# Copies for depthwise convolutions that carry a pair of row shifts per transfer

## The chip, the cores and the metric

The kernel runs on one core of one Trainium2 chip. The metric is the device time of one execution in microseconds. The kernel before took 11327.4 us, the median of three runs (11325.69 to 11348.05).

## The reference

A batch of 64 images of 96 channels and 28 x 28 pixels passes four layers.

```python
# layer 0 (k = 5): routed experts; layers 1 and 3 (k = 3): the same shape without routing and gating
out = act(bn1(conv1x1(x, 96 -> 576)))           # silu in layer 0, relu in layers 1 and 3
out = act(bn2(depthwise_conv(out, k x k)))      # layer 0: a kernel per image, mixed from 4 experts
...                                             # layer 0: squeeze-and-excite gate on out
x   = x + bn3(conv1x1(out, 576 -> 96))          # layer 0: weights mixed from 4 experts
# layer 2, on each quarter (14 x 14) of the image: group norm, conv1x1, 3 x 3 depthwise,
# four-direction selective scan, group norm, gate, channel gate, x + y
```

The depthwise convolutions of layers 0, 1 and 3 work on 576 channels of 28 x 28 pixels: for each channel, the sum over the k x k taps of a shifted image times a weight.

## The kernel before

**Depthwise convolution as matmuls.** TensorE (PE) does it. A tile `rep` holds, on (k + 1) * cb partitions, cb channels in k + 1 row shifts each (cb = 16 and k = 5, 96 partitions; cb = 32 and k = 3, 128 partitions), for n = 4 (or 2) blocks of channels in the free dimension. The rows of an image are split into even and odd ones, two *slots* `o` of 14 rows, each padded to 16 rows of 32 pixels. With k + 1 row shifts and a weight tile `wd`, a matmul sums the taps of all ky at once for even and odd output rows; the k values of dx are k matmuls that accumulate in one bank of PSUM. The weight tile is made of the taps (`_taps`, lines 98 to 107: one row per lane) and a 0/1 `mask` that says which channel a lane belongs to (`spread_taps`, lines 520 to 529; a lane is a partition of `rep`). Channel and shift of a lane are thus set in three places: the copies into `rep`, the taps, and the mask. Before the change a lane is c * (k + 1) + i, for channel c of the block and shift i.

**From the first convolution to the second.** `expand` (lines 634 to 700) computes the 1x1 convolution of four tiles of 128 channels and one of 64. ScalarE (ACT) evicts each half from PSUM into a bordered tile `pad` in SBUF (128 partitions, 2 slots, 16 rows, 32 pixels), and issues a DMA that stores the tile to the HBM scratch tensor `ex` (lines 670 to 674, 128 rows of 4096 bytes); the fifth tile goes through `hpad` in two stores of 64 channels (`store`, lines 690 to 695, rows of 896 bytes). For k = 3 the slots are stored in reversed order (line 643). There are three tensors `ex`, one for each of the layers 1, 0 and 3 in the loop (line 615), whose last 64 channels are zeroed once in setup.

**The copies.** `rows` (lines 702 to 711) fills `rep` from `ex` with k + 1 DMAs on SyncE's (SP's) queue, one for each row shift i: it reads slot i % 2 from row (i + (k == 3)) // 2 on, 14 rows (1792 bytes), of cb channels in n blocks, and writes the partitions i, i + k + 1, i + 2(k + 1) and so on. `load` (lines 713 to 741) asks for this and for the weight tile `wd`: for layer 0, GpSimd (POOL) spreads the mixed taps of the image (line 735); for layers 1 and 3 a DMA loads tiles that setup spread once (line 738). `depthwise` (lines 743 to 803) has the matmuls (line 756) and the evictions (line 767) of such a unit. An image has 9 units in layer 0 and 5 in each of layers 1 and 3, the last of them with n = 2. `rep` has three buffers, `wd` three, PSUM tiles five (lines 426 to 448).

**The rest.** Layer 2's scans run on VectorE (DVE, lines 1268 to 1278), their sums and products on GpSimd (lines 1231, 1297, 1303), and TensorE collects the states (line 1211). `dd`, `B` and `C` come to it through HBM by SP's DMAs (line 1188). The projections (line 825) end in an addition to `x` on DVE (line 837).

**What sets the order.** A planner in the program (`Plan`, lines 237 to 396) simulates all engines when the kernel is built. Each operation is registered with an engine, an estimated cost, its inputs and outputs, and a due time; `run` places operations greedily by the time they can start and by due time, and emits the instructions of every engine in that order. SP's and ACT's DMAs are such operations, with a cost for the issue, a size and a time to land. On the chip each engine takes its own instructions strictly in that order and waits on semaphores. The image loop (lines 1457 to 1461) runs seven times over a body of eight planned slots; in a slot, layer 2 of one image runs beside layer 1 of the next, layer 0 of the one after that, and layer 3 of the previous one.

Of the kernel before, what the change touches and what calls it, by code (L numbers as in the profile page):

```python
# [9 lines left out]
F32 = mybir.dt.float32  # L10
# [5 lines left out]
P = 128  # L16
C = 96
HID = 576
# [56 lines left out]
def _rows(v):  # L75
    return np.tile(np.asarray(v)[None, :], (P, 1))
# [15 lines left out]
def _parity(cb):  # L92

    lane = np.arange(P) // cb % 2
    return 0.5 * np.stack([lane == 0, lane == 1], axis=1).astype(np.float32)


def _taps(w, cb):


    k = w.shape[1]
    v = w.reshape(HID // cb, cb, k, k)
    out = np.zeros((cb, k + 1, HID // cb, k, 2), np.float32)
    for o in range(2):
        for ky in range(k):
            out[:, ky + o, :, :, o] = v[:, :, ky].transpose(1, 0, 2)
    return out.reshape((k + 1) * cb, HID // cb, k, 2)


def pack_l0(ins):  # L110
    q = {k[len("L0_conv_") :]: np.asarray(v) for k, v in ins.items() if k.startswith("L0_conv_")}
    p = Pack()
    p.add("r_w1", q["r_w1"].T)
    p.add("r_b1", q["r_b1"][:, None])
    p.add("r_w2", q["r_w2"].T)
    p.add("r_b2", _rows(q["r_b2"]))
    p.add("w1", q["exp_w"].T)
    _pack_bn(p, "bn1", q, "bn1_g", "bn1_b", "bn1_m", "bn1_v", _lanes)
    _pack_bn(p, "bn2", q, "bn2_g", "bn2_b", "bn2_m", "bn2_v", lambda a: _groups(a, 16))

    dw = np.zeros((96 + RH, E, 360), np.float32)
    for e in range(E):
        dw[:96, e] = _taps(q["dw_w"][e].reshape(HID, 5, 5), 16).reshape(96, 360)
    dw.reshape(96 + RH, E * 360)[96:, : NG * P] = _groups(q["se_w2"], 16).transpose(2, 1, 0).reshape(RH, NG * P)
    p.add("dw", dw)
    p.add("mask", np.repeat(np.eye(16, dtype=np.float32), 6, axis=0))
    p.add("parity", _parity(16))
    p.add("se_w1", _groups(q["se_w1"].T, 16))
    b1 = np.zeros((96 + RH, 1), np.float32)
    b1[96:, 0] = q["se_b1"]  # L130
    p.add("se_b1", b1)
    p.add("se_b2", _groups(q["se_b2"], 16))
    p.add("bn3gr", _rows(q["bn3_g"]), once=True)
    p.add("bn3vr", _rows(q["bn3_v"]), once=True)
    _pack_bn(p, "bn3", q, "bn3_g", "bn3_b", "bn3_m", "bn3_v", None)
    return p
# [8 lines left out]
def pack_l1(ins, layer):  # L145
    pre = f"L{layer}_conv_"
    q = {k[len(pre) :]: np.asarray(v) for k, v in ins.items() if k.startswith(pre)}
    p = Pack()
    p.add("w1", q["w1"][:, :, 0, 0].T)
    _pack_bn(p, "bn1", q, "g1", "b1", "m1", "v1", _lanes)  # L150
    p.add("dw", _taps(q["wd"].reshape(HID, 3, 3), 32).reshape(P, 18 * 6), once=True)
    p.add("mask", np.repeat(np.eye(32, dtype=np.float32), 4, axis=0), once=True)
    _pack_bn(p, "bn2", q, "g2", "b2", "m2", "v2", _lanes)
    p.add("w3", _lanes(q["w3"][:, :, 0, 0].T))
    p.add("bn3gr", _rows(q["g3"]), once=True)
    p.add("bn3vr", _rows(q["v3"]), once=True)
    _pack_bn(p, "bn3", q, "g3", "b3", "m3", "v3", None)
    return p
# [44 lines left out]
PE, ACT, DVE, POOL, SP = "PE", "ACT", "DVE", "POOL", "SP"  # L203
# [218 lines left out]
class Kernel:  # L422
# [4 lines left out]
        rep=(3, [P, 4, 14, 32]),  # L427
        wd=(3, [P, 768]),
        acc=(15, [P, HALF]),
        h=(2, [P, 4, LSEQ]),  # L430
# [100 lines left out]
    def setup(self, fold):  # L531
        nc = self.nc
# [12 lines left out]
        for e in range(E):  # L545
            t = fold.tile([P, NG, C], F32, name="expert")
# [5 lines left out]
        for layer, c in ((1, c1), (3, c3)):  # L552
            k = f"l{layer}"
            bn1 = self.bn(c, "bn1", 1e-5, k)
            bn2 = self.bn(c, "bn2", 1e-5, k)
            _, b3 = self.bn(c, "bn3", 1e-5, k)
# [3 lines left out]
            for u in range(5):  # L560
                n = 24 if u < 4 else 12
                t = fold.tile([P, 768], F32, name="taps")
# [49 lines left out]
        self.hpad = self.tile([P, 2, 7, 32], "hborder")  # L612
        for t in self.pads + [self.hpad]:
            nc.gpsimd.memset(t, 0.0)
        self.ex = [self.dpool.tile([HID, 2, 16, 32], F32, name=f"ex{i}") for i in range(3)]
        for t in self.ex:
            nc.sync.dma_start(t[4 * P :].rearrange("c o r w -> c (o r w)"), self.pads[0][:64].rearrange("c o r w -> c (o r w)"))
        self.npad = self.ndecay = 0

# [2 lines left out]
    def job(self, layer, t, ex):  # L622

        if layer == 0:
            d = dict(c=self.c[0], bn1=self.bn1_0, bn2=self.bn2_0, b3=self.b3_0)
        else:
            d = self.ir[layer]
        k, cb, func, table = (5, 16, AF.Silu, SILU) if layer == 0 else (3, 32, AF.Relu, None)
        return dict(
            d, layer=layer, x=self.xt[t % 4], keys=[("x", t % 4, h) for h in range(2)],  # L630
            k=k, cb=cb, func=func, table=table, ex=self.ex[ex], exkey=ex, accs=[],
        )

    def expand(self, d):


        nc, pl, x, ex = self.nc, self.plan, d["x"], d["ex"]
        pl.tag = d["layer"]
        w1 = d["c"]("w1")
        scale, bias = d["bn1"]  # L640

        def evict(dst, ps, t):
            dst = dst[:, ::-1] if d["k"] == 3 else dst
            nc.scalar.activation(  # L644
                dst,
                ps()[:, :HALF].rearrange("p (r o w) -> p o r w", o=2, w=28),
                d["func"],
                bias=bias[:, t : t + 1],
                scale=scale[:, t : t + 1],
            )  # L650

        for t in range(4):
            i = self.npad % len(self.pads)
            self.npad += 1
            pad = self.pads[i]
            for h in range(2):
                ps = pl.buf("ps")

                def mm(ps=ps, t=t, h=h):
                    nc.tensor.matmul(  # L660
                        ps()[:, :HALF], w1[:, t * P : t * P + P], x[:, h * HALF : (h + 1) * HALF], start=True, stop=True
                    )

                pl.op(PE, 0.68, mm, r=d["keys"], w=[ps], after=[("pad", i, h)])
                pl.op(
                    ACT, 0.68, lambda ps=ps, t=t, h=h, pad=pad: evict(pad[:, :, 1 + 7 * h : 8 + 7 * h, 2:30], ps, t),
                    r=[ps], w=[("pad", i, h)], table=d["table"],
                )
            flat = "p o r w -> p (o r w)"
            pl.op(  # L670
                ACT, 0.35,
                lambda t=t, pad=pad: nc.scalar.dma_start(ex[P * t : P * t + P].rearrange(flat), pad.rearrange(flat)),
                r=[("pad", i, 0), ("pad", i, 1)], w=[("ex", d["exkey"], t)], nbytes=524288, land=3.5,
            )
            yield
            pl.tag = d["layer"]

        ps, pad = pl.buf("ps"), self.hpad

        def mm():  # L680
            for h in range(2):
                nc.tensor.matmul(
                    ps()[64 * h : 64 * h + 64, :HALF],
                    w1[:, 4 * P :],
                    x[:, h * HALF : (h + 1) * HALF],
                    start=True,
                    stop=True,
                )

        def store():  # L690
            for h in range(2):
                nc.scalar.dma_start(
                    ex[4 * P :, :, 1 + 7 * h : 8 + 7 * h].rearrange("p o r w -> p o (r w)"),
                    pad[64 * h : 64 * h + 64].rearrange("p o r w -> p o (r w)"),
                )

        pl.op(PE, 0.68, mm, r=d["keys"], w=[ps], after=["hpad"])
        pl.op(ACT, 0.68, lambda: evict(pad[:, :, :, 2:30], ps, 4), r=[ps], w=["hpad"], table=d["table"])
        pl.op(ACT, 0.7, store, r=["hpad"], w=[("ex", d["exkey"], 4)], nbytes=230000, land=3.2)
        yield  # L700

    def rows(self, d, rep, ch, n):

        nc, k, cb = self.nc, d["k"], d["cb"]
        src = d["ex"][ch : ch + n * cb].rearrange("(b c) o r w -> c b o (r w)", b=n)
        for i in range(k + 1):
            slot, row = i % 2, (i + (k == 3)) // 2
            nc.sync.dma_start(  # L708
                rep()[i : (k + 1) * cb : k + 1, :n].rearrange("c b r w -> c b (r w)"),
                src[:, :, slot, 32 * row : 32 * row + 448],  # L710
            )

    def load(self, d, u):

        nc, pl, k, cb, layer = self.nc, self.plan, d["k"], d["cb"], d["layer"]
        pl.tag = layer
        if layer == 0:
            ch, n = 64 * u, 4
        else:
            ch, n = P * u, 4 if u < 4 else 2  # L720
        rep, wd = pl.buf("rep"), pl.buf("wd")
        pl.op(
            SP, 0.64 * (k + 1), lambda: self.rows(d, rep, ch, n),
            r=[("ex", d["exkey"], ch // P)], w=[rep], nbytes=(k + 1) * cb * n * 1792, land=4.2 if n == 4 and k == 3 else 2.8,
        )
        m = n * k * 2
# [9 lines left out]
        else:  # L736
            pl.op(
                SP, 0.55, lambda: nc.sync.dma_start(wd()[:, : m * cb], self.taps[layer][u][:, : m * cb]),
                w=[wd], nbytes=P * m * cb * 4,
# [753 lines left out]
```

## Time and profile before

| | |
|---|---|
| median of three runs | 11327.4 us |
| the profiled execution | 11346.26 us |
| its span, first to last instruction | 11344.5 us |
| mean granted TensorE clock | 0.896 |
| DMA issues on SP for `rep` | 6016 |
| DMA busy share of the 16 engines, SP's queue / ACT's queue | 50.1% / 12.6% |
| HBM read / written | 1725.77 MB / 539.49 MB |

The profile is one execution. "PE" is TensorE's matmuls and "PEld" its weight loads. In a group's line stand the source line, the engine, the operation, the tiles (`out<-in`), the shape and the count, then busy time in us and the mean of one in ns, then the idle time of the engine just before these instructions and what ended most of it. A view of waits gives, for each pair of waiter and releaser, the total in us, the number of waits and the longest. "SPq" and "ACTq" are DMA issues on SP's and ACT's queues. The granted clock is the share of TensorE's full speed. The trace also holds a record of every DMA packet (queue, size, start, duration) and of every semaphore update; where the text speaks of records, it means these.

### The profile page before, as it was taken

Reading aid. Unit: us, or ns where it says so; the run is one execution under the profiler, and the core shown is the slowest. Engines: PE = TensorE matmul, PEld = TensorE weight load, DVE = VectorE, ACT = ScalarE, POOL = GpSimd, SP = SyncE. Lnnn points to the kernel's source line nnn. Section 1 sums busy time; section 2 is a strip of 40 time slices with the busy share of each in tenths; the row PEclk is TensorE's granted clock in tenths of the full one; section 3 lists DMA queues with packets and bytes.
Section 4 is the critical chain, followed back from the end, with each engine's and each line's share of the span. In section 5 each row is a group of like instructions: output and inputs, shape, how many; then the busy total and the mean of one; then the engine's idle time right before and its main releaser. Section 6 shows DMA issues by size and latency. Waiting matters only on the chain. (4 is left out here: it accounts for less than half of the span.)

```text
span 11344.5 us, 201157 instructions
## 1 busy us (share of the span) xinstructions
PE 9815.9 (87%) x75526; PEld 4055.5 (36%) x75526; DVE 9261.7 (82%) x8711; ACT 6387.5 (56%) x10605; POOL 8342.3 (74%) x7523
## 2 busy tenths in 40 slices
PE   4689888899989899889998988889988898888895
PEld 2233333333333333333333333333333333333332
DVE  1589887889878888788888888888887888888886
ACT  1365555556555565555555655555555665555653
POOL 5477776777767777687786777777777777767786
PEclk9799998899988999898898999889888899989996
DMA  4366665666656666666666666666666666666662
GB/s 144 120 216 205 220 208 190 204 212 212 215 189 206 205 210 212 194 211 209 205 216 197 211 205 214 205 192 216 208 202 194 215 210 211 212 193 208 217 225 97
DMA packets 1114986, 2278.94 MB, mean 201 GB/s; under 512 B 154064, under 2 KB 808144, under 8 KB 1113872
## 3 DMA queue, kind: packets, MB, share of 16 engines
q1 hardware_dynamic: 925008, 1750.19, 50.1%
q10 hardware_dynamic: 188992, 515.69, 12.6%
q8 instruction: 609, 9.98, 0.4%
q14 instruction: 377, 3.09, 0.1%
HBM read 1725.77 MB, written 539.49 MB: 200 GB/s over the span
## 5 line engine op out<-in xcount | busy, mean ns | idle before, releaser
L756 PE MATMUL ps<-rep,wd 128*32 128x392 f32 (+1 forms) x50688 | 5150.1, 547 | 806.5 <-DMA rep<-ex 445.7
L1297 POOL TENSOR_TENSOR yc<-h,g 128x392 f32<-128x392 f32 x1536 | 1955.5, 1296 | 1815.7 <-DVE g L1278 1227.3
L756 PEld LDWEIGHTS ps<-rep,wd 128*32 128x32 f32 (+1 forms) x50688 | 1767.6, 116 | 3709.4 <-issue 2754.8
L1273 DVE TENSOR_TENSOR_SCAN h<-decay,b 128x788 f32<-128x788 f32 x1536 | 2756.9, 1795 | 286.5 <-ACT decay L1250 132.4
L1278 DVE TENSOR_TENSOR_SCAN g<-decay,b 128x788 f32<-128x788 f32 x1536 | 2724.9, 1774 | 0.0
L767 ACT ACTIVATE acc<-ps,l_bn2b,l_bn2s 128x392 f32<-128x392 f32 x1728 | 1152.2, 674 | 2785.0 <-PE ps L756 2565.6
L1268 DVE TENSOR_TENSOR b<-dd,B 128x784 f32<-128x784 f32 x1536 | 2419.3, 1575 | 60.5 <-DMA dd<-ddd 18.6
L1231 POOL TENSOR_TENSOR g<-h,g 128x394 f32<-128x394 f32 x1536 | 1767.0, 1171 | 290.0 <-DVE g L1278 290.0
L1231 POOL TENSOR_TENSOR yc<-yc,C 128x392 f32<-128x392 f32 x1536 | 1826.6, 1209 | 0.0
L660 PE MATMUL ps<-x,blob 96*128 96x392 f32 x3072 | 1387.3, 584 | 187.1 <-DVE x L837 88.4
L1250 ACT ACTIVATE decay<-dd,A 128x784 f32<-128x784 f32 x1536 | 1370.7, 942 | 203.6 <-DVE g L1278 136.1
L1303 POOL TENSOR_TENSOR yc<-yc,g 128x392 f32<-128x392 f32 x1536 | 1443.1, 960 | 0.0
L644 ACT ACTIVATE border<-ps,l_bn1b,l_bn1s 128x392 f32<-128x392 f32 x1536 | 1003.9, 678 | 653.2 <-PE ps L660 599.2
L524 POOL TENSOR_TENSOR wd<-kern,blob 96x640 f32<-96x640 f32 x576 | 834.6, 1453 | 397.4 <-PE ps L756 372.9
L825 PE MATMUL ps<-acc,blob 128*96 128x392 f32 (+1 forms) x2560 | 865.9, 518 | 11.4 <-ACT border L644 10.8
L660 PEld LDWEIGHTS ps<-x,blob 96*128 96x128 f32 x3072 | 589.3, 211 | 784.9 <-issue 269.2
L825 PE MATMUL ps<-acc,wp 128*96 128x392 f32 x2304 | 778.2, 496 | 23.3 <-DVE wp L965 23.1
L1211 PE MATMUL y<-yc,blob 128*32 128x392 f32 x3072 | 461.7, 512 | 149.0 <-POOL yc L1231 149.0
L1250 ACT ACT_TABLE_LOAD x349 | 447.8, 1283 | 251.1 <-DMA dd<-ddd 222.1
L837 DVE SCALAR_TENSOR_TENSOR x<-ps,l_bn3b,x 96x392 f32<-96x392 f32 x384 | 224.2, 610 | 412.0 <-PE ps L825 412.0
L825 PEld LDWEIGHTS ps<-acc,blob 128*96 128x96 f32 (+1 forms) x2560 | 355.4, 166 | 489.6 <-issue 446.8
L825 PEld LDWEIGHTS ps<-acc,wp 128*96 128x96 f32 x2304 | 371.2, 163 | 429.1 <-issue 392.4
(145 smaller groups left out, 7485.4 us busy)
## 6 DMA issues: line engine op xcount, KB each, us to landing
rep<-ex SPq DMA_DIRECT2D x2048, 224.0 KB, 4.2
rep<-ex SPq DMA_DIRECT2D x3968, 112.0 KB, 3.5
ex<-border ACTq DMA_DIRECT2D x768, 512.0 KB, 3.6
dd<-ddd SPq DMA_DIRECT2D x384, 588.0 KB, 5.2
wd<-taps SPq DMA_DIRECT2D x512, 384.0 KB, 4.2
B<-bcd SPq DMA_DIRECT2D x256, 392.0 KB, 4.4
C<-bcd SPq DMA_DIRECT2D x256, 392.0 KB, 4.4
expert<-w SPq DMA_DIRECT2D x256, 240.0 KB, 4.4
```

Of the source, the lines that this page charges most:

```text
L644: nc.scalar.activation(dst, ps()[:, :HALF].rearrange("p (r o w) -> p o r w", o=2, w=28), d["func"], bias=bias[:, t : t + 1], scale=scale[: ...
L660: nc.tensor.matmul(ps()[:, :HALF], w1[:, t * P : t * P + P], x[:, h * HALF : (h + 1) * HALF], start=True, stop=True)
L756: nc.tensor.matmul(ps()[lo : lo + 32, :HALF], w, rep()[: (k + 1) * cb, b, :, 2 - off + dx : 30 - off + dx], start=(dx == 0), stop=(dx == k ...
L767: nc.scalar.activation(acc()[lo : lo + n], ps()[lo : lo + n, :HALF], d["func"], bias=bias[lo : lo + n, at : at + 1], scale=scale[lo : lo + ...
L825: nc.tensor.matmul(banks[o]()[:C, :HALF], w, a, start=(i == 0), stop=(i == (8 if d["layer"] == 0 else 4)))
L1231: nc.gpsimd.tensor_tensor(out[:, i : i + n], *(t[:, i : i + n] for t in ins), op)
L1250: nc.scalar.activation(fs[:, :, u, :, :SEQ], d()[:, :2].rearrange("p o (i l) -> p o i l", i=2), AF.Exp, scale=self.A[:, at : at + 1],)
L1268: nc.vector.tensor_tensor(out, v, w, ALU.mult)
L1273: lambda h=h, ff=ff: nc.vector.tensor_tensor_scan(flat(h()), ff, b, 0.0, ALU.mult, ALU.add),
L1278: lambda g=g, ff=ff: nc.vector.tensor_tensor_scan(flat(g())[:, ::-1], ff[:, ::-1], b[:, ::-1], 0.0, ALU.mult, ALU.add),
L1297: nc.gpsimd.tensor_tensor(out[:, i : i + 2], a[:, i : i + 2], b[:, i : i + 2], ALU.add)
L1303: nc.gpsimd.tensor_tensor(t, t, g()[:, i : i + 2, :SEQ], ALU.add)
```

## The change

A DMA into `rep` now carries two row shifts, one from each slot, so that a unit takes (k + 1) / 2 DMAs. In `ex`, the two slots of a channel lie one after the other, 512 elements apart, so (channel, slot) is one dimension of the source; both slots must then be read from the same row on.

- `rows`: for a pair i, 2 * cb adjacent partitions are written, in the order channel, slot; every pair reads 14 rows from stored row i on. Sizes in bytes are the same.
- For k = 3 the slots needed different rows. So `send` stores 15 rows of each slot, the second slot from its second row on (two runs of 1920 bytes a partition where there was one of 4096), and `store` shifts the second slot's place in the same way. For k = 5 `send` names the slots separately and stores the same bytes.
- `_pairs` brings taps and mask into the new order of lanes: pair, channel, slot.
- Since a k = 3 layer now stores another layout than layer 0, there is one tensor `ex` for each (index, k), six in place of three, and six zero fills in setup.
- The planner's cost of a unit's copies is 0.32 * (k + 1) where it was 0.64 * (k + 1).

```diff
+def _pairs(a, cb):
+
+    rest = a.shape[1:]
+    return a.reshape(cb, -1, 2, *rest).swapaxes(0, 1).reshape(-1, *rest)
...
-    return out.reshape((k + 1) * cb, HID // cb, k, 2)
+    return _pairs(out.reshape((k + 1) * cb, HID // cb, k, 2), cb)
...
-    p.add("mask", np.repeat(np.eye(16, dtype=np.float32), 6, axis=0))
+    p.add("mask", _pairs(np.repeat(np.eye(16, dtype=np.float32), 6, axis=0), 16))
...
-        self.ex = [self.dpool.tile([HID, 2, 16, 32], F32, name=f"ex{i}") for i in range(3)]
-        for t in self.ex:
+        self.ex = {(i, k): self.dpool.tile([HID, 2, 16, 32], F32, name=f"ex{i}_{k}") for i in range(3) for k in (3, 5)}
+        for t in self.ex.values():
...
-            flat = "p o r w -> p (o r w)"
+            def send(t=t, pad=pad):
+                src, dst = (v.rearrange("p o r w -> p o (r w)") for v in (pad, ex[P * t : P * t + P]))
+                if d["k"] == 3:
+
+                    src = bass.AP(src.tensor, src.offset, [src.ap[0], [512 + 32, 2], [1, 480]])
+                    dst = dst[:, :, :480]
+                nc.scalar.dma_start(dst, src)
+
             pl.op(
-                ACT, 0.35,
-                lambda t=t, pad=pad: nc.scalar.dma_start(ex[P * t : P * t + P].rearrange(flat), pad.rearrange(flat)),
+                ACT, 0.35, send,
                 r=[("pad", i, 0), ("pad", i, 1)], w=[("ex", d["exkey"], t)], nbytes=524288, land=3.5,
             )
...
-                nc.scalar.dma_start(
-                    ex[4 * P :, :, 1 + 7 * h : 8 + 7 * h].rearrange("p o r w -> p o (r w)"),
-                    pad[64 * h : 64 * h + 64].rearrange("p o r w -> p o (r w)"),
-                )
+                dst = ex[4 * P :, :, 1 + 7 * h : 8 + 7 * h].rearrange("p o r w -> p o (r w)")
+                if d["k"] == 3:
+                    dst = bass.AP(dst.tensor, dst.offset, [dst.ap[0], [512 - 32, 2], [1, 224]])
+                nc.scalar.dma_start(dst, pad[64 * h : 64 * h + 64].rearrange("p o r w -> p o (r w)"))
...
-        src = d["ex"][ch : ch + n * cb].rearrange("(b c) o r w -> c b o (r w)", b=n)
-        for i in range(k + 1):
-            slot, row = i % 2, (i + (k == 3)) // 2
+        src = d["ex"][ch : ch + n * cb].rearrange("(b c) o r w -> (c o) b (r w)", b=n)
+        for i in range((k + 1) // 2):
             nc.sync.dma_start(
-                rep()[i : (k + 1) * cb : k + 1, :n].rearrange("c b r w -> c b (r w)"),
-                src[:, :, slot, 32 * row : 32 * row + 448],
+                rep()[2 * cb * i : 2 * cb * (i + 1), :n].rearrange("l b r w -> l b (r w)"), src[:, :, 32 * i : 32 * i + 448]
             )
...
-            SP, 0.64 * (k + 1), lambda: self.rows(d, rep, ch, n),
+            SP, 0.32 * (k + 1), lambda: self.rows(d, rep, ch, n),
```

More of the change, by code (lines that the diff above doesn't have):

```diff
@@ L151, in pack_l1 @@
     p.add("dw", _taps(q["wd"].reshape(HID, 3, 3), 32).reshape(P, 18 * 6), once=True)
-    p.add("mask", np.repeat(np.eye(32, dtype=np.float32), 4, axis=0), once=True)
+    p.add("mask", _pairs(np.repeat(np.eye(32, dtype=np.float32), 4, axis=0), 32), once=True)
     _pack_bn(p, "bn2", q, "g2", "b2", "m2", "v2", _lanes)
@@ L630, in job @@
             d, layer=layer, x=self.xt[t % 4], keys=[("x", t % 4, h) for h in range(2)],
-            k=k, cb=cb, func=func, table=table, ex=self.ex[ex], exkey=ex, accs=[],
+            k=k, cb=cb, func=func, table=table, ex=self.ex[ex, k], exkey=(ex, k), accs=[],
         )
```

## The prediction

> **What bounds the kernel now.** I read the page first, then the loop by stretches, then the waits of PE and of SP's queue, then one stretch of the timeline.
>
> From the page, the engines and the costliest group:
>
> ```profile
> PE 9815.9 (87%) x75526; PEld 4055.5 (36%) x75526; DVE 9261.7 (82%) x8711; ACT 6387.5 (56%) x10605; POOL 8342.3 (74%) x7523
> ...
> L756 PE MATMUL ps<-rep,wd 128*32 128x392 f32 (+1 forms) x50688 | 5150.1, 547 | 806.5 <-DMA rep<-ex 445.7
> ```
>
> No engine is full. PE leads, half of its work are the depthwise matmuls (L756), and most of what they wait for are the copies into `rep`. The seven passes of the loop alone (busy us of PE, PEld, DVE, ACT, POOL, then granted clock, DMA share, GB/s):
>
> ```profile
> 1130.00:10640.00 9510.00, 8468.12 (x65457) 3501.17 (x65449) 7989.22 (x7480) 5542.32 (x9197) 7112.29 (x6481) 0.90 0.65 207
> ```
>
> PE is busy 89%, at a clock of 0.90. PE's waits and the longest of SP's queue (us in total, times, longest):
>
> ```profile
> PE ps L756 <- DMA rep<-ex: 445.7, 207, 7.4
> PE y L1211 <- POOL yc L1231: 149.0, 70, 9.2
> ...
> SPq L708 <- DMA ex<-border: 1605.8, 376, 28.9
> SPq L708 <- PE ps L756: 661.1, 170, 8.9
> ```
>
> The first wait is three times the next. SP, which issues these copies, is itself held by stores to `ex`. Why, a stretch of the timeline shows (SP's, ACT's and PE's answers; start, us, engine):
>
> ```profile
> 5073.89 3.75 SPq L708 DMA_DIRECT2D rep<-ex  x6
> ...
> 5094.62 6.89 SPq L708 DMA_DIRECT2D rep<-ex  x6
> ...
> 5097.51 0.34 ACTq L672 DMA_DIRECT2D ex<-border  x1
> ...
> 5103.89 3.57 PE L756 MATMUL ps<-rep,wd 96*32 96x392 f32 x24 [3.97 <-DMA rep<-ex]
> ```
>
> Six copies issue in 3.75 us, or in 6.89: four went out, the fifth did not begin before ACT's store, issued at 5097.51, had landed at 5100.30. That store is no input of the fifth copy, for the first four of the same unit read the same rows. The records show eight semaphores for all DMAs of SP and ACT; each issue waits until the DMA before it on its semaphore has landed. I counted 801 of SP's stalls (1623 us) that end within 0.12 us of such a landing; 1122 us of them are a `rep` copy behind a store to `ex`. So a unit's six issues are a train that any late store can stop.
>
> By unit (the trace's records, matmuls matched to their copies): of 576 layer 0 units, 275 start on PE after idling and within 0.6 us of the last landing; they idle 601 us (more than the page's 446, which counts only waits whose last releaser was the copy). Of the 640 units of layers 1 and 3, 50 start within 1.5 us of their landing, half of all about 5 us or more after it.
>
> **The change, part by part.**
>
> *Issues.* Now 6 x 9 (layer 0) and 4 x 10 (layers 1, 3) copies an image, then 3 x 9 and 2 x 10: 6016 become 3008.
>
> ```profile
> L708 SPq DMA_DIRECT2D rep<-ex x6016: 554/594/2834, 147.8 to 11325.2; - x195
> L672 ACTq DMA_DIRECT2D ex<-border x768: 321/327/624, 145.2 to 11308.3; - x192
> L692 ACTq DMA_DIRECT2D ex<-hborder x384: 514/613/2212, 147.7 to 11301.5; - x192
> ```
>
> (min/median/max ns.) A copy of 64 rows takes 593 ns of SP, one of 128 rows 602, so I take 0.6 us for 256 rows too; if the 9 ns grew in proportion, 0.62. SP saves 3008 x 0.6 = 1800 us, a layer 0 unit 3 x 0.64 = 1.9 us of its train, a layer 1 or 3 unit 1.25. With 9629 DMAs on eight semaphores the DMA waited for was issued 8 x 11344/9629 = 9.4 us earlier on average; with 6621 it is 13.7 us, well over a store's 3.6 us landing. I take half of the stalls inside trains as gone; the ends are none and all.
>
> *Landing.* Bytes and row size (1792 B) stay, but a copy now writes 64 (layer 0: 32) adjacent partitions instead of every fourth (sixth). Here the rows speak against the change (KB each, us to landing, both from the quiet setup):
>
> ```profile
> taps<-taps SPq DMA_DIRECT2D x8, 384.0 KB, 2.4
> ...
> ex<-border SPq DMA_DIRECT2D x3, 256.0 KB, 3.1
> ```
>
> The second reads 64 adjacent partitions, the first 128, and less takes longer. The packet records say by how much: 4096-byte packets of the 64-partition transfers take 267 ns on average, those of ACT's 128-partition stores 167, a factor of 1.6. Applied to a 1792-byte packet (74 ns at the median), that is +44 ns. An engine carries 24 of them for a layer 0 unit and 32 for the others: +1.06 and +1.41 us. So a layer 0 unit lands 1.9 - 1.06 = 0.84 us earlier and a layer 1 or 3 unit 0.16 us later. DMA engines are busy 516096 x 44 ns / 16 = 1420 us more, 0.65 to 0.78 in the loop. Ends: no loss (reading is not writing, and the transfers of a unit use different partitions), and a doubling of the present mean of 94 ns.
>
> [...]
>
> *What PE gets back.* For each of the 275 units I take the smaller of its wait and (half of its train's excess over 3.75 us, plus 0.84 us): 461 us in all. With no stall recovered it is 208, with all 526.
>
> *Clock.* The granted clock is halved in 324 stretches, 2354 us in all. In 121 of them (655 us) the longest PE idle in the 6.9 us before is a `rep` wait. At PE's 89% a half clock costs 655 x 0.5 x 0.89 = 291 us; with 461 of 601 us of waits gone, 224 return. If the two only happen to coincide, this term is nothing. [...]
>
> *How much reaches the end.* 461 + 224 = 685 us of PE time, but PE is not alone. DVE idles 2083 us, of which 972 end with a PE result (`u` 437, `x` 412, `ps` 123); POOL idles 3002 us, of which 941 do (445, 373, 107, 16). That is 47% and 31%; I let 39% through: **-267 us**. What is late next is the scan chain on DVE and POOL (L1297 waits 1227 us for DVE).
>
> *Costs.* Of 768 stores to `ex`, the 512 of layers 1 and 3 become two runs a partition, as in L692: +0.29 us each, 146 us of ACT's queue. ACT waits 2566 us for PE at L767, which covers most; I take 20, at the ends 0 and 219 (layer 0's too, and no cover). Their bytes fall by 6%, but twice the packets at half the time is no gain. Three more zero fills in setup: 2 us. DMA engines 13 points busier: some 110 waits for other loads grow by 0.5 us, times 0.39, 20 us. Later layer 1 and 3 units: 50 x 0.16, 8 us. Together **+50**.
>
> *Order.* The planner is told half of SP's cost, so it emits every engine's work in another order. The trace prices this only in size: slots 2 to 7 of each pass do equal work in different planned orders and take 161 to 175 us, about 3 us of spread; over eight slots 1 us in 168, so 0.6% or 70 us, of either sign. I take zero.
>
> **Sum.** The profiled execution took 11346.3 us (span 11344.5). 11346 - 267 + 50 = 11129. It was 19 us above the median of the three runs (11327.4), so I forecast **11110 us**.
>
> **Rivals.**
> *The ports decide, and it is slower* (0.13). If the mean packet goes from 94 to 188 ns, the copies take 3030 us more engine time and the share reaches 0.92. Layer 0 units land 0.35 us later (275 x 0.35 = 96 us), the others 1.8 later (some 75 without that slack, 0.9 each, 70), and 110 waits on other loads grow by 1.5 (165). With halved clock on top, half of this reaches the end: about 11480. For: setup's 298 ns median against 159. Against: there one transfer ran alone. It decides from 94 + 1900/24 = 173 ns on; for layers 1 and 3 already from 133.
> *The plan spends the gain* (0.20). It now expects layer 0's tiles 1.9 us earlier; they come 0.84 earlier, so PE is sent to them early and waits as before. That the plan has no semaphores and already sends PE to 275 of 576 units on their landing speaks for it. Then the order's 70 us remain: 11260 to 11400, about 11330.
> *The trains were all of it* (0.12). All stalls gone, 526 us and 255 of clock, and 60% reaches the end, as PE leads: 11327 - 470 = 10860.
> *The forecast* has 0.55, with 10980 to 11260 as its own range.
>
> **Range and chances.** 10880 to 11440 takes in the forecast and most of the second and third rival. Two kernels can be told apart by about 0.2%. Faster by more than that: most of 0.55, all of 0.12, a little of the second rival, 0.70; within it 0.07; slower 0.23.
>
> **What would show it.** Right: 3008 copies at about 0.6 us, PE's wait for `rep` under 250 us, SP's waits at L708 for `ex` halved, layer 0 units' first issue to last landing down from 7.7 us, clock above 0.90. The 1792-byte packets' mean near 138 ns and a DMA share near 0.78 test the landing step; a mean under 110 makes the gain larger, over 173 makes it slower. Wrong: waits on `rep` as long as now with the copies landing earlier (the plan), or issues that grow with the rows (SP saves nothing).

## The result, and the profile after

The kernel after takes **11416.3 us** (median of four runs, 11398.0 to 11419.7), against 11326.6 us for the kernel before in the same session (four runs, 11325.3 to 11348.1). The ratio is 1.0071, with a 95% interval of 1.0054 to 1.0089: 0.7% slower. Its profiled execution took 11398.0 us (span 11396.2, mean clock 0.898). The forecast was 11110; the range held the time, the sign was wrong.

The page of after, engines, two groups of instructions and DMA issues (KB each, median us from issue to landing):

```profile
PE 9666.1 (85%) x75526; PEld 4056.6 (36%) x75526; DVE 9517.0 (84%) x8711; ACT 6456.7 (57%) x10631; POOL 8286.9 (73%) x7523
...
L768 PE MATMUL ps<-rep,wd 128*32 128x392 f32 (+1 forms) x50688 | 4992.8, 532 | 600.3 <-DMA rep<-ex 181.1
L1280 DVE TENSOR_TENSOR b<-dd,B 128x784 f32<-128x784 f32 x1536 | 2674.1, 1741 | 67.9 <-DMA dd<-ddd 27.1
...
rep<-ex SPq DMA_DIRECT2D x1024, 448.0 KB, 8.5
rep<-ex SPq DMA_DIRECT2D x1984, 224.0 KB, 5.0
ex<-border ACTq DMA_DIRECT2D x512, 480.0 KB, 7.3
dd<-ddd SPq DMA_DIRECT2D x384, 588.0 KB, 7.7
wd<-taps SPq DMA_DIRECT2D x512, 384.0 KB, 6.7
```

The same DMA rows of the kernel before:

```profile
rep<-ex SPq DMA_DIRECT2D x2048, 224.0 KB, 4.2
rep<-ex SPq DMA_DIRECT2D x3968, 112.0 KB, 3.5
ex<-border ACTq DMA_DIRECT2D x768, 512.0 KB, 3.6
dd<-ddd SPq DMA_DIRECT2D x384, 588.0 KB, 5.2
wd<-taps SPq DMA_DIRECT2D x512, 384.0 KB, 4.2
```

The wait that the change was to shorten did get shorter: 445.7 us before (L756 there), 181.1 now. But most large transfers take longer to land: the stores of layers 1 and 3 to `ex` 7.3 us where all 768 had 3.6, `dd` 7.7 for 5.2, `wd` 6.7 for 4.2. The 256 one-run stores of layer 0 do not (3.0 us). (The 1024 copies of 448 KB are units of layers 1 and 3 with four blocks; the 1984 others are layer 0's and those of two blocks.) The loop's 9510 us, as above with clock, DMA share and GB/s at the end, and the waits of PE:

```profile
1130.00:10640.00 9510.00, 8288.60 (x65076) 3474.27 (x65075) 8208.37 (x7443) 5578.43 (x9171) 7034.40 (x6453) 0.90 0.74 204
```

```profile
PE ps L768 <- DMA rep<-ex: 181.1, 79, 9.3
PE ps L768 <- DMA wd<-taps: 155.9, 49, 6.0
PE ps L1058 <- DVE gs L1046: 127.7, 48, 21.5
...
PE ps L837 <- ACT border L650: 73.3, 47, 3.9
```

The clock has not risen (0.90 in the loop, as before). 264 us of waits for `rep` are gone; `wd` from HBM takes 156 us where it took 28. Summed over all its lines, PE's idle time that ended with ACT grew from 154 to 478 us and that with DVE from 489 to 621, while that with POOL fell from 309 to 174. SP's queue:

```profile
SPq L721 <- PE ps L768: 1688.2, 506, 16.4
SPq L721 <- DMA ex<-border: 1424.9, 264, 35.7
```

SP now waits longest for PE to free a buffer of `rep`; its waits for stores went from 1605.8 us to 1424.9, not to half.

So the copies' own wait shrank, and the time grew. Two suspects were left: the new copies cost more elsewhere than they save, or the planner's halved cost, which re-orders all engines, costs more than they save.

### The profile page after: what moved, and what is told of

It is laid out like the page before. It is cut to its first block, busy times and chain, and to the rows that moved or that the text cites. A ratio compares the mean times of both kernels' runs of the same rounds, so it can differ in the third digit from the quotient of the medians.

```text
span 11396.2 us, 196337 instructions
## 1 busy us (share of the span) xinstructions
PE 9666.1 (85%) x75526; PEld 4056.6 (36%) x75526; DVE 9517.0 (84%) x8711; ACT 6456.7 (57%) x10631; POOL 8286.9 (73%) x7523
## 5 line engine op out<-in xcount | busy, mean ns | idle before, releaser
L768 PE MATMUL ps<-rep,wd 128*32 128x392 f32 (+1 forms) x50688 | 4992.8, 532 | 600.3 <-DMA rep<-ex 181.1
L768 PEld LDWEIGHTS ps<-rep,wd 128*32 128x32 f32 (+1 forms) x50688 | 1742.8, 114 | 3337.1 <-issue 2670.4
L1309 POOL TENSOR_TENSOR yc<-h,g 128x392 f32<-128x392 f32 x1536 | 1886.7, 1251 | 1173.6 <-DVE g L1290 1003.0
L1280 DVE TENSOR_TENSOR b<-dd,B 128x784 f32<-128x784 f32 x1536 | 2674.1, 1741 | 67.9 <-DMA dd<-ddd 27.1
L1243 POOL TENSOR_TENSOR g<-h,g 128x394 f32<-128x394 f32 x1536 | 1850.3, 1225 | 800.4 <-DVE g L1290 799.2
L1243 POOL TENSOR_TENSOR yc<-yc,C 128x392 f32<-128x392 f32 x1536 | 1713.3, 1136 | 0.0
L666 PE MATMUL ps<-x,blob 96*128 96x392 f32 x3072 | 1418.5, 596 | 245.7 <-DVE rw L905 76.1
L1315 POOL TENSOR_TENSOR yc<-yc,g 128x392 f32<-128x392 f32 x1536 | 1493.9, 993 | 0.0
L837 PE MATMUL ps<-acc,blob 128*96 128x392 f32 (+1 forms) x2560 | 892.6, 530 | 78.7 <-ACT border L650 73.3
L1064 POOL TENSOR_TENSOR gs<-gs,mhalf 96x2 f32<-96x2 f32 x256 | 195.5, 763 | 681.3 <-ACT gs L1061 668.3
```

Source lines behind the costliest of these rows:

```text
L666: nc.tensor.matmul(ps()[:, :HALF], w1[:, t * P : t * P + P], x[:, h * HALF : (h + 1) * HALF], start=True, stop=True)
L768: nc.tensor.matmul(ps()[lo : lo + 32, :HALF], w, rep()[: (k + 1) * cb, b, :, 2 - off + dx : 30 - off + dx], start=(dx == 0), stop=(dx == k ...
L837: nc.tensor.matmul(banks[o]()[:C, :HALF], w, a, start=(i == 0), stop=(i == (8 if d["layer"] == 0 else 4)))
L1243: nc.gpsimd.tensor_tensor(out[:, i : i + n], *(t[:, i : i + n] for t in ins), op)
L1280: nc.vector.tensor_tensor(out, v, w, ALU.mult)
L1309: nc.gpsimd.tensor_tensor(out[:, i : i + 2], a[:, i : i + 2], b[:, i : i + 2], ALU.add)
```

## Experiments

### Copies and order apart

Theory **C**: the copies are at fault (adjacent partitions, two-run stores, queues); the expectations call it B and name ports, which no run looks at. Theory **O**: the order is; the expectations call it A. The edit of the cost can be made without the edit of the copies, and the other way round. With cost 0.64 and the new copies, PE, DVE, ACT and POOL run their instructions in the sequence of the kernel before, instruction by instruction; with 0.32 and the old copies, in the sequence of the kernel after. That makes a table of two by two.

```diff
 # new_copies_old_order: after, but
-            SP, 0.32 * (k + 1), lambda: self.rows(d, rep, ch, n),
+            SP, 0.64 * (k + 1), lambda: self.rows(d, rep, ch, n),
 # old_copies_new_order: before, but
-            SP, 0.64 * (k + 1), lambda: self.rows(d, rep, ch, n),
+            SP, 0.32 * (k + 1), lambda: self.rows(d, rep, ch, n),
```

Two more kernels keep the pairs but write partitions (k + 1) / 2 apart instead of adjacent ones, with lanes in the order channel, pair, slot: `spread_old_order` with cost 0.64, `spread_new_order` with 0.32.

```diff
+        m = (k + 1) // 2
...
-                rep()[2 * cb * i : 2 * cb * (i + 1), :n].rearrange("l b r w -> l b (r w)"), ...
+                rep()[i : 2 * cb * m : m, :n].rearrange("l b r w -> l b (r w)"), ...
...
-    return a.reshape(cb, -1, 2, *rest).swapaxes(0, 1).reshape(-1, *rest)
+    return a.reshape(cb, -1, 2, *rest).swapaxes(1, 2).reshape(-1, *rest)
```

> The change in full, but the planner is told the cost of before (0.64 in place of 0.32 per row shift), so that PE, DVE, ACT and POOL run the instructions of the kernel before in exactly its order; only the DMAs differ. Theory A (the new order lost what the copies gained): PE's wait for rep stays near 180 us, DVE's busy time goes back from 9517 to about 9260 us, and the time is 1 to 2% under before, 11100 to 11220 us. Theory B (the copies themselves lose, by shared partitions' ports and longer queues in the DMA engines): the mean 1792-byte packet stays near 124 ns, and the time is at or above that of the change, 11400 us or more.

> The copies of before, one row shift each, but the planner is told the cost of the change, so that PE, DVE, ACT and POOL run in exactly the order of the changed kernel. Theory A: the order alone loses, the time is 1 to 2.5% above before, 11440 to 11600 us, DVE busy near 9500 us. Theory B: the order is worth nothing or even gains, 11250 to 11350 us.

> New copies in the order of before, with lanes laid out so that the partitions of a copy lie 2 (layer 0: 3) apart over all 128 (96) instead of adjacent; bytes, rows and issues are those of the change. Theory B: the mean 1792-byte packet falls from 124 to about 95 ns, layer 1 and 3 copies land in about 5 us instead of 8.5, and the time is at least 1% under new_copies_old_order. Theory A: landings get shorter too, but the time differs from new_copies_old_order by under 0.4%, since PE waits for few copies.

> The same spread lanes in the order of the changed kernel. Theory B: at least 1% under the change, 11300 us or less. Theory A: within 0.4% of the change, 11370 to 11460 us.

| median us, ratio to before (95%) | order of before (0.64) | order of after (0.32) |
|---|---|---|
| old copies | 11327.5 | 12099.1, 1.0675 (1.0648 to 1.0702) |
| new copies, adjacent | 10830.1, 0.955 (0.9527 to 0.9574) | 11416.3, 1.0071 (from the first session) |
| new copies, spread | 10637.6, 0.940 (0.9376 to 0.9423) | 11249.6, 0.9932 (0.9910 to 0.9954) |

In equal order the new copies take 497 us off. The new order costs 5.4% with them (11416.3 / 10830.1), 5.8% with spread ones and 6.8% with the old ones. The diff holds a gain of 4.5% and a loss of 5.4%, and the result is their sum. Theory O holds, though both sizes were missed: 10830 was to be at least 11100, and 12099 at most 11600. C falls as a whole; a part of it, the adjacent partitions, costs 1.8% (10830.1 / 10637.6), and there C's figure (at least 1%) came true and O's (under 0.4%) did not.

The loop, waits of PE and SP's longest wait in `new_copies_old_order`:

```profile
1130.00:10640.00 9510.00, 8553.44 (x68514) 3594.42 (x68514) 8618.42 (x7896) 5822.94 (x9664) 7573.79 (x6850) 0.93 0.78 215
```

```profile
PE ps L768 <- DMA wd<-taps: 212.4, 53, 7.0
PE y L1223 <- POOL yc L1243: 160.3, 73, 9.2
PE ps L768 <- DMA rep<-ex: 125.7, 82, 6.4
...
PE ps L837 <- ACT border L650: 15.0, 13, 2.1
...
SPq L721 <- DMA ex<-border: 1607.2, 241, 30.0
```

The same copies, the other order: DVE is busy 410 us more of the 9510, the clock is 0.93 instead of 0.90, and PE's wait for ACT's `border` is 15 us instead of 73. Summed over all lines, PE's idle time that ended with ACT is 196 us here and 478 in after, with DVE 481 and 621, with DMA 411 and 371, with POOL 211 and 174: 345 us more idle in after, spread over many lines, and 655 us more at half clock (2320 against 1665).

And `old_copies_new_order`, its waits and its loop:

```profile
PE ps L756 <- DMA rep<-ex: 500.9, 179, 9.2
PE ps L756 <- DMA wd<-taps: 240.1, 44, 11.3
```

```profile
1130.00:10640.00 9510.00, 7964.43 (x60778) 3312.44 (x60778) 7600.98 (x6955) 5197.78 (x8569) 6556.91 (x6032) 0.88 0.59 192
```

PE, DVE and POOL are less busy than in before. The waits for `rep` and `wd` are 267 us longer there (501 + 240 against 446 + 28), of 772 us that were lost: the rest is again spread over waits of the engines for each other.

### Why does the order cost?

Theory **P** (from the prediction's second rival): with cost 0.32 the planner promises tiles sooner than they come, and sends PE to them early. Theory **O**, sharpened: the old order is one of a few good ones, and nearly any other loses. First, the two things that the cost means to the planner, how long SP is taken and when the tile arrives, can be changed one at a time (both kernels have the new copies). Then the cost can be changed by 3%, which changes the promise by 0.08 to 0.12 us.

```diff
 # plan_free_same_arrival: cost 0.32, and the arrival put back
-... land=4.2 if n == 4 and k == 3 else 2.8,
+... land=(4.2 if n == 4 and k == 3 else 2.8) + 0.32 * (k + 1),
 # plan_held_early_arrival: cost 0.64, and the arrival earlier
+... land=(4.2 if n == 4 and k == 3 else 2.8) + -0.32 * (k + 1),
 # plan_cost_062 and plan_cost_066: after, but
-            SP, 0.32 * (k + 1), lambda: self.rows(d, rep, ch, n),
+            SP, 0.62 * (k + 1), lambda: self.rows(d, rep, ch, n),
```

> The new copies; the planner is told the halved cost on SP's queue, but that the tiles land as late after the start as before (0.32 per row shift added to the landing). SP is free earlier, nothing is promised earlier. Theory P: within 1% of new_copies_old_order, 10720 to 10940 us. Theory O: 3 to 6% above it, 11150 to 11480 us.

> The new copies; the planner is told the old cost on SP's queue, but landings 0.32 per row shift earlier (1.3 us for a layer 1 or 3 unit, 1.9 for layer 0), that is the promise of the change alone. Theory P: as slow as the change, 11350 to 11480 us. Theory O: 11150 to 11480 us too, but then the other three runs are as slow.

> The new copies, planner's cost 0.62 per row shift in place of 0.64: SP's issue of a unit is thought 0.08 or 0.12 us shorter, 3%. The emitted order still differs from that of before in a third of PE's places. Theory P (promise: the order is bad because the planner expects the tiles 1.3 to 1.9 us too early): this promises next to nothing more, so the time stays within 1% of new_copies_old_order, 10720 to 10940 us. Theory O (the due times fit one order only, and any other order loses): 3 to 6% above it, 11150 to 11480 us.

> The new copies, planner's cost 0.66: a unit's issue is thought 3% longer, so tiles are expected later and not earlier. Theory P: within 1% of new_copies_old_order or faster, 10700 to 10900 us. Theory O: 3 to 6% above it, 11150 to 11480 us.

| new copies, planner told | median us | ratio to before (95%) | to the order of before (10830) |
|---|---|---|---|
| SP free early, arrival as at 0.64 | 11279.0 | 0.9941 (0.9918 to 0.9965) | +4.1% |
| SP held as at 0.64, arrival early | 11534.8 | 1.0166 (1.0134 to 1.0198) | +6.5% |
| cost 0.62 | 11610.7 | 1.0245 (1.0214 to 1.0276) | +7.2% |
| cost 0.66 | 11668.8 | 1.0280 (1.0244 to 1.0317) | +7.7% |

P falls: a promise changed by a tenth of a microsecond costs more than the halved one, and in both directions. A cost of 0.62 gives another place to a third of PE's instructions, about as many as 0.32 does (of the 9452 instructions that the program holds for PE, 6292 to 6724 keep their place with 0.62 and 0.66, 6054 with 0.32). O holds, and three of the four lie above the 3 to 6% that it gave. What is lost is the particular sequence.

The planner has a table `DUE` of 114 numbers, each a shift of the due time of one kind of operation (`op` adds it to the time that the caller asks for). Without it, theory O expects the old order's lead to shrink.

```diff
-DUE = (
-    -5, 7, -10, 6, -7, 0, 15, -24, -32, -22, 22, 26, -1, -19, 7, 1, -1, 16, -28, -35, 10, -4, 35, -40, -16,
...
+DUE = ()
```

> New copies, the table of due-time corrections (114 hand-written numbers) emptied, planner's cost 0.64. Theory O': it is this table that fits one order; without it the cost 0.64 gives no better order than another, so this run and no_due_cost_032 lie within 3% of each other and both well above 10830 us, 11300 to 11900. Rival: the cost 0.64 is the better number in itself (nearer to what a unit's copies take with their stalls); then this run stays 4 to 6% under no_due_cost_032.

> New copies, the table of due-time corrections emptied, planner's cost 0.32. Theory O': within 3% of no_due_cost_064, 11300 to 11900 us. Rival: 4 to 6% above it.

With cost 0.64 it takes 11402.2 us (ratio 1.0046, 1.0027 to 1.0065), with 0.32 11605.6 (1.0231, 1.0189 to 1.0273). The table is worth 5.3% at 0.64 (11402 / 10830) and 1.7% at 0.32 (11606 / 11416). So without the table the gap between the two costs falls from 5.4% to 1.8%: most of the old order's lead goes with the table. That the table fits this one sequence is the likely reading; it rests on one order at each cost. Which instructions' places carry the loss isn't settled: no run moved one queue alone. One part can be counted in the traces. ACT loads a table of functions in 1.28 us, 1132 times in the old order, 1158 in that of after, and 1170, 1276, 1236 and 1224 times in the four kernels of the table above, which is 33 to 185 us more of ACT's time. It is not the whole: without `DUE`, at cost 0.64, there are 1139 loads and the loss is 5.3%.

### Which copies gain, and what adjacent partitions cost

From here on every kernel has the order of before (cost 0.64). Theory **L**: layer 0 carries the gain, since its units wait; layers 1 and 3, which had 50 units near their landing, can only lose. The pairing is made for one value of k at a time:

```diff
+PAIRED = (5,)     # layer0_only, layer0_spread; (3,) in layers13_only, layers13_spread
...
-    return _pairs(out.reshape((k + 1) * cb, HID // cb, k, 2), cb)
+    out = out.reshape((k + 1) * cb, HID // cb, k, 2)
+    return _pairs(out, cb) if k in PAIRED else out
...
-                if d["k"] == 3:
+                if d["k"] == 3 and 3 in PAIRED:
...
+        if k not in PAIRED:
+            ...                       # the k + 1 copies of before
+            return
```

The two "spread" kernels write partitions (k + 1) / 2 apart in the paired layers, as above.

> Old order, paired copies in layer 0 alone (27 instead of 54 copies an image); layers 1 and 3 keep one copy per row shift, their one-run stores and their lanes. Theory L (the prediction's step: PE's waits for rep are layer 0's, so its shorter trains bring the gain): 10800 to 10950 us, nearly all of the 497 us that both together brought in this order. Rival S (what counts is the load on SP's queue and on the eight DMA semaphores, whichever layer's copies go): 27 of 47 copies, 11000 to 11100 us.

> Old order, paired copies in layers 1 and 3 alone (20 instead of 40 copies an image, with the two-run stores). Theory L: within 1% of before, 11250 to 11400 us. Rival S: 20 of 47 copies, 11080 to 11180 us.

> Old order, paired copies in layers 1 and 3 alone as in layers13_only, but a copy's 64 partitions lie 2 apart instead of adjacent. Theory R (the loss of 0.8% in layers13_only is the shared ports): the mean packet falls from 118 to about 95 ns and the time to 11330 us or less. Rival T (it is the two-run stores, or copies that now start together and queue): within 0.4% of layers13_only, 11385 to 11475 us.

> Old order, paired copies in layer 0 alone as in layer0_only (10651 us), with the 32 partitions of a copy 3 apart instead of adjacent. Theory R: the mean packet falls from 106 to about 93 ns and the time by a further 0.3 to 1%, 10540 to 10620 us. Rival: 32 partitions wait for little, 10630 to 10670 us.

| paired, order of before | median us | ratio (95%) | layer 0 units waiting, us | packet of 1792 B, mean ns | DMA share |
|---|---|---|---|---|---|
| none (before) | 11327 | 1 | 275, 601 | 94 | 0.65 |
| layer 0, adjacent | 10650.9 | 0.9388 (0.9353 to 0.9422) | 96, 134 | 106 | 0.72 |
| layer 0, spread | 10632.2 | 0.9381 (0.9358 to 0.9404) | 80, 101 | 98 | 0.70 |
| layers 1 and 3, adjacent | 11430.8 | 1.0078 (1.0052 to 1.0104) | 262, 597 | 118 | 0.72 |
| layers 1 and 3, spread | 11314.4 | 0.9991 (0.9974 to 1.0007) | 285, 568 | 91 | 0.63 |
| all, adjacent | 10830.1 | 0.955 (0.9527 to 0.9574) | 93, 139 | 124 | 0.78 |
| all, spread | 10637.6 | 0.940 (0.9376 to 0.9423) | 68, 95 | 96 | 0.68 |

L holds: layer 0 alone gives 6.1%, more than the whole, and more than the 10800 to 10950 us that L expected. For layers 1 and 3 the page shows what the adjacent partitions cost. `layers13_only`, then `layers13_spread`:

```profile
rep<-ex SPq DMA_DIRECT2D x1024, 448.0 KB, 7.2
...
wd<-taps SPq DMA_DIRECT2D x512, 384.0 KB, 6.7
```

```profile
rep<-ex SPq DMA_DIRECT2D x1024, 448.0 KB, 5.3
...
wd<-taps SPq DMA_DIRECT2D x512, 384.0 KB, 5.1
```

Same bytes, same number of copies, same rows: 64 adjacent partitions land in 7.2 us, 64 partitions two apart in 5.3, and `wd`, on the same queue, in 6.7 and 5.1. This is worth 0.9% of the time (1.0078 to 0.9991). In layer 0, where a copy writes 32 partitions, adjacent or three apart can't be told apart. The median 1792-byte packet takes 74 ns in before, 131 in after, 74 with spread partitions. What the runs vary is the place of the partitions; none looks at a port, so the "shared ports" of theory R are the author's guess at the cause.

### The two-run stores

What do layers 1 and 3 lose otherwise, that fewer issues don't help them? One kernel has only their new stores and keeps the k + 1 copies, which then all start at stored row i // 2. A second adds the three further zero fills to before.

```diff
 # two_run_stores: after with cost 0.64, PAIRED = (), and the stores of k = 3 kept; its copies
+                slot, row = i % 2, i // 2
 # three_more_fills: before, with
+        more = [self.dpool.tile([64, 2, 16, 32], F32, name=f"more{i}") for i in range(3)]
+        for t in more:
+            nc.sync.dma_start(t.rearrange("c o r w -> c (o r w)"), self.pads[0][:64].rearrange("c o r w -> c (o r w)"))
```

> Old order, one copy per row shift everywhere as before; only the stores of layers 1 and 3 are those of the change (two runs of 1920 bytes a partition instead of one of 4096, ACT's issue 0.53 us instead of 0.33), and the copies read the shifted rows. Theory T: half or more of the loss of layers13_only, 11370 us or more. Theory R: within 0.3% of before, 11300 to 11375 us.

> The kernel before with three more zero fills of 256 KB in setup, as the change has them, into tensors that nothing reads; every later DMA then uses a semaphore three places on. If the loss of two_run_stores (0.6%) comes from the setup or from which semaphore a DMA gets: 11380 to 11430 us. If it is the stores themselves: 11320 to 11350 us.

The stores cost 0.6%: 11403.4 us, ratio 1.0062 (1.0042 to 1.0083). The fills cost nothing that shows: 1.0014 (0.9996 to 1.0032). ACT's store takes 0.52 us to issue instead of 0.33:

```profile
L685 ACTq DMA_DIRECT2D ex<-border x768: 326/521/1567, 149.9 to 11384.8; - x192
```

(min/median/max ns; of the 768, the 256 of layer 0 stay short.) 512 x 0.2 = 102 us of ACT's queue. How this reaches the time isn't shown. PE's wait for `rep`, whose copies wait for these stores, is 559.0 us against 445.7 in before, but in `three_more_fills`, which is no slower than before, it is 531.7 (the first line is of `two_run_stores`, the second of `three_more_fills`):

```profile
PE ps L779 <- DMA rep<-ex: 559.0, 255, 6.8
```

```profile
PE ps L759 <- DMA rep<-ex: 531.7, 236, 7.3
```

So with spread partitions the fewer issues of layers 1 and 3 just pay for the stores.

### What the gain of layer 0 consists of

Is it the fewer issues, or the larger transfers? `layer0_only`, with a small DMA ahead of each paired copy (64 runs of 64 bytes, from HBM to one of eight scratch tensors), has six issues and six semaphores a unit again. The scratch tensors are read by nothing.

```diff
+        self.few = [self.dpool.tile([16, 4, 32], F32, name=f"few{i}") for i in range(8)]
...
+            few = self.few[self.nfew % 8]
+            self.nfew += 1
+            nc.sync.dma_start(few[:, :, :16], self.taps[1][0][:16, :64].rearrange("p (a b) -> p a b", a=4))
             nc.sync.dma_start(
```

> layer0_only with one small DMA of the old shape (64 runs, of 64 bytes) ahead of each paired copy of layer 0, so that SP issues six DMAs a unit again and the eight semaphores turn as fast as before, while the bytes of the copies do not change. Theory L (the trains: issues and semaphores) : most of the gain of 677 us goes, 11100 to 11400 us. Rival: the gain is in the transfers themselves and stays, 10650 to 10800 us.

It takes 11011.1 us, ratio 0.9717 (0.9692 to 0.9743), between the two expectations. Of the 6.1 points 3.3 are given back, and PE waits for `rep` twice as long as in `layer0_only`; the first line is of `layer0_only`, the second of `layer0_small_extra`:

```profile
PE ps L779 <- DMA rep<-ex: 123.4, 83, 7.5
```

```profile
PE ps L783 <- DMA rep<-ex: 250.4, 122, 7.9
```

More than half of layer 0's gain is thus the number of issues. A unit's train (first issue to the end of the last) takes 4.44 us at the median in before, 1.63 in `layer0_only`, 3.25 here. The rest isn't settled: the kernel doesn't undo all of it, since a unit's train stays 1.2 us shorter than in before, though the small DMAs land no sooner (3.51 us at the median) than the copies of 16 partitions in before (3.33).

### A version without the costs

If stores and adjacent partitions are what layers 1 and 3 lose, a pairing without them should not lose: shifts 1 and 2 read the same stored row of the two slots even with the one-run stores of before, so they can share a copy (64 partitions, two apart), while shifts 0 and 3 go alone. Three copies a unit, layer 0 as in `layer0_spread`. The taps of layers 1 and 3 are put into the lanes' new order.

```diff
...
+            nc.sync.dma_start(rep()[0:P:2, :n].rearrange("l b r w -> l b (r w)"), both[:, :, 32:480])
+            for at, slot, row in ((1, 0, 0), (3, 1, 2)):
+                nc.sync.dma_start(
+                    rep()[at:P:4, :n].rearrange("c b r w -> c b (r w)"), src[:, :, slot, 32 * row : 32 * row + 448]
+                )
```

> Old order, layer 0 as in layer0_spread; in layers 1 and 3 only the two row shifts that start in the same stored row (shifts 1 and 2) go in one copy of 64 partitions 2 apart, shifts 0 and 3 stay single, so that three copies of four remain and the stores keep one run. If issues of layers 1 and 3 are worth what layers13_spread gained over two_run_stores (89 us for two copies fewer a unit): half of that under layer0_spread, 10570 to 10610 us. If they are worth nothing once layer 0 is paired: 10620 to 10660 us.

It takes 10606.2 us, ratio 0.9369 (0.9344 to 0.9394), the lowest here. The median lies in the range for "the issues of layers 1 and 3 are worth something" (10570 to 10610) and not in the other, but against `layer0_spread` (0.9381) the intervals overlap: whether the fewer copies are worth a little or nothing can't be told. Both take over 6% less than before and about 7% less than after.

## Why the prediction was wrong, point by point

**Order: this step failed.** "The trace prices this only in size ... so 0.6% or 70 us, of either sign. I take zero." It was not nothing: it cost 586 us (11416 less 10830), against 497 us that the copies gave in equal order, and so the sign turned. The spread of slots 2 to 7 came from parts of one plan, all placed under the same table of due times, and says nothing about plans that the table doesn't fit. Every other sequence that was run with the new adjacent copies, seven of them, took 4.1% to 7.7% longer than the old one. Nor was the sign open: none gained.

**Second rival, "The plan spends the gain".** Its range, 11260 to 11400, ends 16 us short of the time, and it is right that the plan decides; its mechanism, tiles promised too early, fell (a cost of 0.62 or 0.66 loses more).

**What PE gets back: the number right by luck, the mechanism not.** 461 us were predicted. In equal order layer 0's waits fall from 601 us to 139, by 462; the prediction's mark, PE's wait for `rep` under 250 us, is met in both orders (126 and 181). But the units were to land sooner after their first issue, since half of the stalls behind stores would go away and the train would be shorter. At the median they don't: in equal order a layer 0 unit needs 7.97 us from first issue to last landing, 7.72 in before (6.73 in after), and SP's wait for stores at these copies, to be halved, is 1607.2 us against 1605.8. What moved is the start. The records put a unit's first issue 11.36 us (median) ahead of the moment when PE ends the work before it, 9.06 us in before, 11.24 in `layer0_only` and 8.66 in `layer0_small_extra`, where units wait 397 us again. That SP comes to each unit sooner because it spends less time on issues fits this; the prediction had no such term.

**Clock: low.** 224 us predicted. Half-clock time falls from 2354 to 1665 us in equal order: 689 x 0.5 x 0.89 = 307. In after it is 2320: what the copies gave, the new order took back. The prediction put part of the half-clock time down to PE's waits. The runs with the most and the least of it agree: 3006 us at half clock in `old_copies_new_order` (PE idle 2191 us) and 1498 in `layers13_three_copies` (idle 1169). Before and after do not follow it: 2354 us with 1529 idle, 2320 with 1730. So the sum of idle time alone does not set it.

**How much reaches the end: low.** 39% predicted. PE got back 462 + 307 = 769 us, and 497 reached the end after all costs, 65%. The share was read from who ended DVE's and POOL's idle time, which counts only the last link of each wait, a likely reason that no run tests; in equal order both speed up with PE (DVE from 7989 to 8618 us of the loop's 9510, POOL from 7112 to 7574).

**Issues: right in kind.** 3008, as counted. SP's time for them falls from 3769 to 1538 us, by 2231 and not 1800, since layer 0's copies take 0.42 us at the median. The trains fell more than thought, from 4.44 to 1.71 us.

**Landing: right for the quickest layer 0 units only.** The packet's mean was to be 138 ns and the share 0.78; they are 124 and 0.78 in equal order (0.74 in after, where the pace is lower). A layer 0 unit was to land 0.84 us earlier after its first issue. In equal order the quickest tenth does (within 5.03 us against 5.96), but the median unit lands 0.25 us later (7.97 against 7.72): its train is 2.7 us shorter, and from last issue to last landing it takes 5.02 us where it took 2.02. And units of layers 1 and 3, to land 0.16 us later, need 8.40 us from first issue to last landing instead of 6.57, and 9.40 in after. The estimate set the longer packets against the shorter train. What else holds a unit's last copy back isn't shown. In after, `wd` went from 4.2 to 6.7 us, `dd` from 5.2 to 7.7, and PE's wait for `wd` from 28 to 156 us: the "+20 us for other loads" was too small.

**Costs of the stores: low.** 20 us within the ends of 0 and 219; measured 0.6%, some 70 us. The queue time is not the reason (102 us against 146 expected); why ACT's slack did not cover it stays open.

**First and third rival.** The first had the sign, by another cause: the adjacent partitions cost 1.8% of the time, and with them the copies still gain 4.5% in equal order. No run looks at the ports that it names. In layer 0 alone, with the partitions spread, 10632 is below the 10860 of "the trains were all of it".

## What to carry to other kernels

When a change edits code and a planner's cost together, build the two edits apart: an equal order of instructions prices the code, and here the code was worth -4.5% and the order +5.4%. A schedule that a table of corrections shapes can lose its lead with a small change of one cost (here over 7% for one of 3%), so expect to fit the table again when a cost is corrected, or leave the cost as it was. When DMAs are merged, spread the written partitions over SBUF (worth 1.8% here), keep the stores that feed them in one run (0.6%), and merge only where something waits for the train (with adjacent partitions, layer 0 alone took 10650.9 us and all layers 10830.1).

## What the runs showed that was not expected

- A copy into 32 adjacent partitions issues in 0.42 us at the median in after and in `layer0_only` (0.30 at the least), in 0.58 behind the small DMAs of `layer0_small_extra`. Copies into 64 adjacent partitions take 0.59 us (128 rows) and 0.60 (256 rows) in after, those of before 0.59 (64 rows) and 0.60 (128 rows).
- A change of 3% in one planned cost moved the time by 7%, more than removing the whole table of due times (5.3%).
- DVE's product of L1280 (L1268 before) takes 1741 ns on average in after, 1709 with the same copies in the old order, 1671 with the old copies in the new order and 1575 in before. The median is 984 ns in all four: the difference is in the long ones. The traces of before and after show what goes with them. With no POOL instruction beside it the product never takes more than 984 ns (32 of the 1536 in before, 79 in after). Of the time of those over 1300 ns, POOL is busy for 91% in before and 95% in after, of the time of the others for 92% and 82%. That POOL holds them up is not tested by a run.
